# Taking the row sums of an attention chunk half a step earlier, its inverse between two clips, and the fetch of the inverse behind the last product

## The chip, the cores and the metric

The kernel runs on one core of a Trainium2 chip. A core has a matrix engine (TensorE, PE in the profile), three engines for elementwise work (VectorE or DVE, ScalarE or ACT, GpSimd or POOL), and SyncE (SP), which here only issues transfers. Each engine takes its own instructions in order, and waits on semaphores that the others raise. TensorE writes to PSUM, a small accumulator memory; the rest lives in SBUF. The metric is the device time of one launch, in microseconds (us).

## The reference

Eight graphs of 2048 nodes with 256 features go through two layers. Each layer normalises its input, clips it at zero, attends and adds the result to the input. Only the first layer is touched here. It has four heads of 64 features. Its softmax isn't taken over all 2048 keys, but within each of eight chunks of 256 keys, and the chunks' results are added:

```
scores = einsum('bhnd,bhjcd->bhnjc', q, kc) / sqrt(Dh)
scores = clip(scores, -10.0, 10.0)
scores = where(mask == 0, -10.0, scores)
attn = softmax(scores, axis=-1)          # over the 256 keys of chunk j
ctx = einsum('bhnjc,bhjcd->bhnd', attn, vc)
out = ctx @ Wo.T + bo + x                # then a layer norm with gamma, beta
```

So each query needs a sum of exponentials for each head and chunk, and each chunk's product with v has to be multiplied by the inverse of that sum before it's added to the others.

## The kernel before, in words

The first layer (`layers`, up to line 724) works in 256 steps: 8 graphs, 4 blocks of 512 queries, 8 chunks of 256 keys. A chunk is two key tiles of 128 keys, `kt` = 2c and 2c + 1. All of it is float32. For one step these instructions run:

- **Scores** (`scores`, line 396): for each key tile and each pair of heads `hp`, two matmuls on the two halves of the array's rows fill one PSUM tile `big` (two buffers). In the trace a matmul of float32 is two records, so the scores of one key tile, both pairs, are 8 records.
- **Clip** (line 404): one VectorE instruction per pair takes `big` through max and min with the mask's limits into an SBUF tile `E` of 128x1024.
- **Exponential** (`exponential`, line 410): ScalarE, in place.
- **Pair sum** (line 680): POOL adds the `E` of the two key tiles of the chunk, for each pair: `add`, two buffers.
- **Sums** (`add_up`, line 427): four matmuls with a block of ones, one per head, each on 32 of the array's columns, sum the pair sums over the keys into PSUM tile `sums`. Heads 0 and 1 read the first pair's `add`, heads 2 and 3 the second's.
- **Inverse** (`divide` and `spread`, lines 434 to 446): ScalarE copies `sums` into `s`; a transfer gathers one row per head into a tile `sum` of 128x16, VectorE takes its reciprocal, a transfer writes it to device memory (`inv`), and four transfers spread each head's row over 32 partitions of `r`, which has one buffer.
- **Products** (`weigh`, line 416): for each key tile and each half `part` of a head's features, four matmuls, one per head, on 32 columns each. Both key tiles accumulate in PSUM tile `both`, which has one buffer.
- **Accumulate** (line 452 on VectorE, line 454 on POOL): `both` times `r` into `c`, and `c` added to `acc`. The first chunk of a block goes to `acc` directly.

These aren't run for one chunk at once. The order is written out by hand in the loop after line 685: at step n TensorE makes the scores of chunk n + 2, sums the pair sums of chunk n + 1 and takes the products of chunk n. A step has two halves, `k` = 0 and 1. In each half come the scores of one key tile of chunk n + 2, then the products of one key tile of chunk n; in the second half the sums of chunk n + 1 stand between the two groups of products. `prepared` is a generator that yields after each part of chunk n + 2, so that its last part (the second pair's exponential and the two pair sums) is issued at the end of the step.

At the end of each half, `advance()` lets waiting side work issue one piece. Side work is: making q, k and v of the next graph (`block`: transposes at line 171, projections at 297 and 191), finishing a block of queries (`finish`: output projection at 479, statistics, normalisation, and POOL's additions at 469 and 512), a graph's statistics, and the start of the second layer. I call the two places slot 1 and slot 2 below, by their order in a step. In `finish`, the step after a block's last chunk runs four ScalarE activations (466) and one POOL addition (469); the next one the output projection in both slots; the one after that a square root (127), for which ScalarE loads another activation table and then loads the exponential's again.

SP issues all the transfers of this layer but the stores of finished blocks, in order: the gather of sums, the write of inverses, the four spreads of `r`, and the loads of x.

The second layer (from line 724) isn't touched.

Of the kernel before, what the change touches and what calls it, by code (L numbers as in the profile page):

```python
# [8 lines left out]
F32 = mybir.dt.float32  # L9
# [7 lines left out]
P = 128  # L17
# [10 lines left out]
def bcast(ap, axis, n):  # L28

    ap = ap.unsqueeze(axis)  # L30
    shape = list(ap.shape)
    shape[axis] = n
    return ap.broadcast_to(shape)
# [18 lines left out]
def layers(  # L52
# [22 lines left out]
    QB = 512  # L75
# [3 lines left out]
    NCH = N // 256  # L79
# [6 lines left out]
    psum = ctx.enter_context(tc.tile_pool(name="psum", bufs=1, space=PSUM))  # L86
# [12 lines left out]
    def heads_tile(name, tag, bufs=2):  # L99
        return big.tile([P, 2, QB], F32, tag=tag, name=name, bufs=bufs)  # L100
# [100 lines left out]
    aside = []  # L201
    here = [0]

    def advance():

        moved = False
        for steps_of in list(aside):
            got = next(steps_of, aside)
            if got is aside:
                aside.remove(steps_of)  # L210
            moved = moved or got is not False
            if got is None:
                break
        return moved

    def drain(until=lambda: False):
        while not until() and advance():
            pass
# [52 lines left out]
    def other_limits():  # L271
        for qb in range(1, NQB):
            yield from make_limit(qb)

    qkv, norm_of = {}, {}
# [43 lines left out]
    def batch(b):  # L319
        qkv[b] = ([], [], [])  # L320
        if b == 0:
            mv, rstd, off = norms()
            norm_of[b] = rstd, off
            for blk, xb in enumerate(ahead(x[b])):
                if blk == 0:
                    yield True
                for t in range(NT):
                    row_stats(nc, small, mv[:, blk * NT + t, :], xb[:, t, :])
                of = slice(blk * NT, (blk + 1) * NT)
                roots(mv, rstd, off, of)  # L330
                offsets(rstd, off, of)
                yield from block(b, blk, xb, *qkv[b])
        else:
            norm_of[b] = yield from statistics(x[b])
            for blk, xb in enumerate(ahead(x[b])):
                yield from block(b, blk, xb, *qkv[b])
# [5 lines left out]
    for name, w in (("q", Wq), ("k", Wk), ("v", Wv), ("o", Wo)):  # L342
# [4 lines left out]
        if name == "o":  # L347

            got = big.tile([P, FC, F], F32, tag="c", name="w_halves")
# [41 lines left out]
    def scores(qb, kt, hp, qs, ks):  # L391

        ps = psum.tile([P, 2, QB], F32, tag="big", name="big", bufs=2)
        for hh in range(2):
            own = slice(hh * DH, (hh + 1) * DH)
            nc.tensor.matmul(  # L396
                ps[:, hh, :],
                ks[kt // NT][own, hp, (kt % NT) * P : (kt % NT + 1) * P],
                qs[qb][own, hp, :],
                start=True,  # L400
                stop=True,
            )
        e = heads_tile("E", "E", 10)
        nc.vector.scalar_tensor_tensor(  # L404
            e, ps, -0.5, bcast(limit[:, qb, kt, :], 1, 2), ALU.max, ALU.min
        )
        return e

    def exponential(e):
        nc.scalar.activation(e, e, AF.Exp, scale=0.25 * EDGE)  # L410

    def weigh(kt, part, es, vs, both, first):

        for h in range(H):
            mine = slice(h * DH + 32 * part, h * DH + 32 * part + 32)
            nc.tensor.matmul(  # L416
                both[32 * h : 32 * h + 32, part, :],
                vs[kt // NT][:, kt % NT, mine],
                es[h // 2][:, h % 2, :],
                start=first,  # L420
                stop=not first,
            )

    def add_up(es, sums):

        for h in range(H):
            nc.tensor.matmul(  # L427
                sums[32 * h : 32 * h + 32, :], ones, es[h // 2][:, h % 2, :], start=True, stop=True
            )

    def divide(sums):

        s = big.tile([P, QB], F32, tag="s", name="s", bufs=1)
        nc.scalar.copy(s, sums)  # L434
        got = small.tile([P, 16], F32, tag="sum", name="sum")
        nc.sync.dma_start(got, s[0:P:32, :].rearrange("h (j i) -> h j i", i=16))
        return got

    def spread(got):

        nc.vector.reciprocal(got, got)
        held = dram.tile([H, QB], F32, tag="inv", name="inv", bufs=3)
        nc.sync.dma_start(held.rearrange("h (j i) -> (h j) i", i=16), got)
        r = big.tile([P, QB], F32, tag="r", name="r", bufs=1)
        for h in range(H):
            nc.sync.dma_start(r[32 * h : 32 * h + 32, :], held[h, :].partition_broadcast(32))
        return r

    def accumulate(acc, both, r, first):

        to = acc if first else heads_tile("c", "c")
        nc.vector.tensor_tensor(to, both, bcast(r, 1, 2), ALU.mult)  # L452
        if not first:
            nc.gpsimd.tensor_tensor(acc, acc, to, ALU.add)  # L454
# [186 lines left out]
    def fill(qb):  # L641

        while here[0] < (B - 1) * NQB * NCH + qb * NCH + NCH - 1:
            yield False
        for two in range(NKT // 2):
            mine = limit[:, qb, 2 * two : 2 * two + 2, :]
            nc.scalar.activation(mine, mine, AF.Relu, scale=2.0 * FULL, saturate=False)
            yield True

    def last_batch():  # L650
        yield from batch(B - 1)
        yield from sources_of(W, a)
        yield from preparation(0)
# [7 lines left out]
    accs = {}  # L661

    def prepared(step):


        b, qb, c = step
        drain(lambda: qb in made and b in qkv and len(qkv[b][1]) > c // 2)
        qs, ks, _ = qkv[b]
        first = [scores(qb, 2 * c, hp, qs, ks) for hp in range(2)]
        for e in first:  # L670
            exponential(e)
        yield first
        second = [scores(qb, 2 * c + 1, hp, qs, ks) for hp in range(2)]
        exponential(second[0])
        yield second
        exponential(second[1])
        added = []
        for hp in range(2):
            both = heads_tile("add", "add")
            nc.gpsimd.tensor_tensor(both, first[hp], second[hp], ALU.add)  # L680
            added.append(both)
        yield added


    weights, rs, got = {}, {}, None
    for n in range(-2, len(steps)):
        here[0] = n
        more = n < NCH - 1
        coming = prepared(steps[n + 2]) if n + 2 < len(steps) else iter(())
        inside = -1 <= n < len(steps) - 1  # L690
        if n >= 0:
            b, qb, c = steps[n]
            if n == 0:
                aside.append(other_limits())
            if (qb, c) == (0, 2) and b + 1 < B:
                aside.append(batch(b + 1) if b + 2 < B else last_batch())
            if b == B - 1 and c == NCH - 2:
                aside.append(fill(qb))
            drain(lambda: len(qkv[b][2]) > c // 2)
            early[0] = False  # L700
            both = psum.tile([P, 2, QB], F32, tag="both", name="both")
        for k in range(2):
            weights.setdefault(n + 2, []).append(next(coming, None))
            if more:
                advance()
            if n >= 0:
                weigh(2 * c + k, 0, weights[n][k], qkv[b][2], both, k == 0)
            if k == 1 and inside:
                sums = psum.tile([P, QB], F32, tag="sums", name="sums")
                add_up(weights[n + 1][2], sums)  # L710
                got = divide(sums)
            if n >= 0:
                weigh(2 * c + k, 1, weights[n][k], qkv[b][2], both, k == 0)
            if k == 0 and got:
                rs[n] = spread(got)
                got = None
            if k == 1:
                weights[n + 2].append(next(coming, None))
                if n >= 0:
                    if c == 0:  # L720
                        accs[qb] = heads_tile("acc", "acc")
                    accumulate(accs[qb], both, rs.pop(n), c == 0)
                    weights.pop(n)
                    if c == NCH - 1:
                        aside.insert(0, finish(b, qb, accs[qb]))
            advance()


    inverse_most = const.tile([P, 4 * B], F32, tag="most", name="most")
# [122 lines left out]
    due, ts, acc, den = [], None, None, None  # L852
    for s, (k, jt) in enumerate(rounds):
        here[0] = len(steps) + s // 4
        b, hp, half = passes[k]
        qn, held, off_s, far, quot, for_sums = shared[b]
# [3 lines left out]
        if jt == 0:  # L860
            acc = psum.tile([P, 2, QB], F32, tag="both", name="acc1")
# [339 lines left out]
```

## Time and profile before

| | |
|---|---|
| median of 3 runs | 4478.36 us (4476.7 to 4484.94) |
| profiled execution | 4470.84 us |
| its span, first to last instruction | 4469.0 us |
| the first layer's steps | about 125 to 2905 us of the span |
| PE busy | 4235.0 us, 95% |
| POOL busy | 3275.9 us, 73% |
| DVE busy | 3157.1 us, 71% |
| ACT busy | 2712.5 us, 61% |

All times of the prediction are from this one profiled execution. A row of the groups is: line, engine, operation, tile written and tile read, shapes, count, busy time, mean of one. In the timeline a row begins with the start in us from the span's start and the length in us, and can hold several instructions of one group; what stands in brackets at its end is the engine's idle time just before, and what ended it. PEld is the load of weights that goes ahead of a matmul. TensorE's ends are modelled, so lengths of consecutive groups of matmuls overlap a little; the distance from one start to the next is the better measure of what a group takes.

### The profile page before, as it was taken

What the parts mean: (1) busy time and instruction counts of PE and PEld (TensorE: products, weight loads), DVE (VectorE), ACT (ScalarE), POOL (GpSimd) and SP (SyncE); (2) the same over time, 40 slices, a digit from 0 to 9 for tenths busy, and PEclk for the clock granted to TensorE, in tenths of its full rate; (3) what the DMA queues carried; (4) which work ended last, traced back from release to release, by engine and by line L of the source; (5) the groups of instructions that cost most, each with busy time, mean ns of one, the idle gap of its engine ahead of it and who ended that gap; (6) DMA issues with size and microseconds to landing.
All of it is one profiled execution on the core that took longest, in us unless ns stands there. A gap on an engine that the chain in (4) does not pass through costs nothing. (4 is left out here: it accounts for less than half of the span.)

```text
span 4469.0 us, 73769 instructions
## 1 busy us (share of the span) xinstructions
PE 4235.0 (95%) x28598; PEld 1462.8 (33%) x28598; DVE 3157.1 (71%) x3736; ACT 2712.5 (61%) x3454; POOL 3275.9 (73%) x1558
## 2 busy tenths in 40 slices
PE   6799999999999999999999999989999999999998
PEld 3233333323323333333333333323233332323332
DVE  1775566566565565575565566588989889898987
ACT  4766556656655665665656557565647566565755
POOL 0477787787677777777777777777877777787877
PEclk8999999999999999999999999999999999999999
DMA  2421121111121121121111122121221212122111
GB/s 70 140 62 44 43 66 47 43 56 56 35 64 54 37 66 44 46 64 44 47 55 50 40 64 61 44 100 50 72 63 60 78 57 86 52 74 62 59 55 35
DMA packets 295000, 262.03 MB, mean 59 GB/s; under 512 B 96240, under 2 KB 245488, under 8 KB 294640
## 3 DMA queue, kind: packets, MB, share of 16 engines
q1 hardware_dynamic: 290032, 240.45, 18.8%
q0 software_dynamic: 4608, 16.78, 1.0%
q8 instruction: 226, 3.70, 0.3%
q14 instruction: 134, 1.10, 0.1%
HBM read 218.83 MB, written 36.18 MB: 57 GB/s over the span
## 5 line engine op out<-in xcount | busy, mean ns | idle before, releaser
L680 POOL TENSOR_TENSOR add<-E 128x1024 f32<-128x1024 f32 x512 | 1201.3, 2369 | 721.9 <-PE sums L427 532.1
L410 ACT ACTIVATE E<-E 128x1024 f32<-128x1024 f32 x1024 | 1080.5, 1057 | 827.3 <-DVE E L404 809.6
L404 DVE SCALAR_TENSOR_TENSOR E<-big,limit 128x1024 f32<-128x1024 f32 x1024 | 1203.7, 1217 | 521.6 <-PE big L396 515.5
L761 DVE SCALAR_TENSOR_TENSOR e<-near,far,limit 128x1024 f32<-128x1024 f32 x1024 | 1240.0, 1273 | 23.2 <-ACT near L750 9.8
L878 POOL TENSOR_TENSOR t<-t,e 128x1024 f32<-128x1024 f32 x448 | 1054.4, 2387 | 246.0 <-ACT t L874 210.4
L416 PE MATMUL both<-E,v 128*32 128x512 f32 x8192 | 1037.7, 601 | 59.8 <-DVE c L452 42.3
L772 PE MATMUL acc<-e,qn 128*32 128x512 f32 x8192 | 1060.7, 597 | 24.4 <-DVE e L761 13.5
L396 PE MATMUL big<-qT,kT 64*128 64x512 f32 x4096 | 1032.3, 620 | 11.8 <-DVE E L404 11.8
L874 ACT ACTIVATE t<-e,quot 128x1024 f32<-128x1024 f32 x512 | 561.2, 1142 | 313.5 <-PE den L784 173.0
L396 PEld LDWEIGHTS big<-qT,kT 64*128 64x128 f32 x4096 | 351.6, 187 | 572.0 <-issue 348.8
L454 POOL TENSOR_TENSOR acc<-acc,c 128x1024 f32<-128x1024 f32 x224 | 532.9, 2379 | 3.6 <-DVE c L452 3.6
L452 DVE TENSOR_TENSOR c<-both,r 128x1024 f32<-128x1024 f32 x224 | 274.2, 1224 | 345.9 <-PE both L416 157.1
L416 PEld LDWEIGHTS both<-E,v 128*32 128x32 f32 x8192 | 214.7, 109 | 752.3 <-issue 572.8
L772 PEld LDWEIGHTS acc<-e,qn 128*32 128x32 f32 x8192 | 259.2, 109 | 591.5 <-issue 451.1
L784 PE MATMUL den<-t,for_sums 128*32 128x512 f32 x2048 | 347.6, 595 | 30.6 <-POOL t L878 29.8
L427 PE MATMUL sums<-add,ones 128*32 128x512 f32 x2048 | 269.1, 592 | 0.2 <-POOL add L680 0.2
L434 ACT COPY s<-sums 128x512 f32<-128x512 f32 x256 | 148.4, 580 | 75.5 <-PE sums L427 71.3
L784 PEld LDWEIGHTS den<-t,for_sums 128*32 128x32 f32 x2048 | 79.2, 110 | 223.1 <-issue 113.3
L191 PE MATMUL aux<-w,hT 128*128 128x256 f32 x512 | 127.6, 392 | 22.6 <-DVE qn L629 22.6
L160 ACT ACTIVATE h<-x,off,rstd 128x256 f32<-128x256 f32 x256 | 139.2, 593 | 4.3 <-DMA x<-in_x_dram 2.3
L297 PE MATMUL aux<-hT,wq 128*128 128x512 f32 x256 | 135.7, 658 | 2.7 <-ACT hT L172 2.7
L479 PE MATMUL aux<-wo,acc 128*128 128x256 f32 x512 | 128.2, 393 | 0.0
(117 smaller groups left out, 3033.8 us busy)
## 6 DMA issues: line engine op xcount, KB each, us to landing
r<-inv SPq DMA_DIRECT2D x1024, 64.0 KB
x<-in_x_dram SPq DMA_DIRECT2D x92, 512.0 KB
x<-x SPq DMA_DIRECT2D x64, 512.0 KB
es<-er SPq DMA_DIRECT2D x64, 512.0 KB
adj_in<-in_adj_dram SPq DMA_DIRECT2D x32, 512.0 KB
x<-o POOLq DMA_DIRECT2D x32, 512.0 KB, 3.9
xh<-x SPq DMA_DIRECT2D x64, 256.0 KB
out_dram<-xh SPq DMA_DIRECT2D x64, 256.0 KB
```

Of the source, the lines that this page charges most:

```text
L396: nc.tensor.matmul(ps[:, hh, :], ks[kt // NT][own, hp, (kt % NT) * P : (kt % NT + 1) * P], qs[qb][own, hp, :], start=True, stop=True,)
L404: nc.vector.scalar_tensor_tensor(e, ps, -0.5, bcast(limit[:, qb, kt, :], 1, 2), ALU.max, ALU.min)
L410: nc.scalar.activation(e, e, AF.Exp, scale=0.25 * EDGE)
L416: nc.tensor.matmul(both[32 * h : 32 * h + 32, part, :], vs[kt // NT][:, kt % NT, mine], es[h // 2][:, h % 2, :], start=first, stop=not first,)
L452: nc.vector.tensor_tensor(to, both, bcast(r, 1, 2), ALU.mult)
L454: nc.gpsimd.tensor_tensor(acc, acc, to, ALU.add)
L680: nc.gpsimd.tensor_tensor(both, first[hp], second[hp], ALU.add)
L761: nc.vector.scalar_tensor_tensor(e, near[hh], far[:, jt, h : h + 1], limit[:, 2 * half : 2 * half + 2, jt, :], ALU.max, ALU.min,)
L772: nc.tensor.matmul(acc[32 * q : 32 * q + 32, blk, :], qn[jt // NT][:, jt % NT, hp * P + 32 * q : hp * P + 32 * q + 32], es[q // 2][:, blk, :],
L784: nc.tensor.matmul(den[32 * q : 32 * q + 32, :], for_sums[:, m, 2 * hp + q // 2, :], ts[q // 2][:, q % 2, :], start=(m == 0 and k == 0), s ...
L874: nc.scalar.activation(t, now[hh], AF.Copy, scale=quot[:, jt // 2, h : h + 1])
L878: nc.gpsimd.tensor_tensor(ts[hh], ts[hh], now[hh], ALU.add)
```

## The change

The loop over `k` is written out, and four things move:

- The sums of chunk n + 1, with the copy and the gather, stand between the two groups of products of the first key tile, not of the second. They come before the exponentials of the first key tile of chunk n + 2, which `prepared` now issues after its first yield.
- The scores of the second key tile are issued in two parts, and the reciprocal and the write of `inv` (now `inverse_of`) stand between them, so that VectorE takes the reciprocal between the clips of the two pairs. Before, they came in the next step, after both clips of its first key tile.
- The products of the second key tile are eight matmuls in a row.
- The four spreads of `r` (`spread`) are issued at the end of the step, after the accumulate of chunk n, which reads the one buffer of `r`. Before, they came in the first half of the step that uses them.

The pair sums stay at the end of the step, and nothing is added or taken away.

```diff
+    def inverse_of(got):
         nc.vector.reciprocal(got, got)
         held = dram.tile([H, QB], F32, tag="inv", name="inv", bufs=3)
         nc.sync.dma_start(held.rearrange("h (j i) -> (h j) i", i=16), got)
+        return held
+
+    def spread(held):
         r = big.tile([P, QB], F32, tag="r", name="r", bufs=1)
...
         first = [scores(qb, 2 * c, hp, qs, ks) for hp in range(2)]
+        yield first
         for e in first:
             exponential(e)
-        yield first
-        second = [scores(qb, 2 * c + 1, hp, qs, ks) for hp in range(2)]
+        yield
+        second = [scores(qb, 2 * c + 1, 0, qs, ks)]
+        yield
+        second.append(scores(qb, 2 * c + 1, 1, qs, ks))
         exponential(second[0])
         yield second
         exponential(second[1])
...
-        for k in range(2):
-            weights.setdefault(n + 2, []).append(next(coming, None))
-            if more:
-                advance()
-            if n >= 0:
-                weigh(2 * c + k, 0, weights[n][k], qkv[b][2], both, k == 0)
-            if k == 1 and inside:
-                sums = psum.tile([P, QB], F32, tag="sums", name="sums")
-                add_up(weights[n + 1][2], sums)
-                got = divide(sums)
-            if n >= 0:
-                weigh(2 * c + k, 1, weights[n][k], qkv[b][2], both, k == 0)
-            if k == 0 and got:
-                rs[n] = spread(got)
-                got = None
...
+        weights[n + 2] = [next(coming, None)]
...
+            weigh(2 * c, 0, weights[n][0], qkv[b][2], both, True)
+        got = held = None
+        if inside:
+            sums = psum.tile([P, QB], F32, tag="sums", name="sums")
+            add_up(weights[n + 1][2], sums)
+            got = divide(sums)
+        next(coming, None)
+        if n >= 0:
+            weigh(2 * c, 1, weights[n][0], qkv[b][2], both, True)
+        advance()
+        next(coming, None)
+        if got:
+            held = inverse_of(got)
+        weights[n + 2].append(next(coming, None))
...
+            for part in range(2):
+                weigh(2 * c + 1, part, weights[n][1], qkv[b][2], both, False)
+        weights[n + 2].append(next(coming, None))
...
+            accumulate(accs[qb], both, r, c == 0)
...
+        if held:
+            r = spread(held)
+        advance()
```

More of the change, by code (lines that the diff above doesn't have):

```diff
@@ L437, in divide @@
         return got
-    def spread(got):
+    def inverse_of(got):
         nc.vector.reciprocal(got, got)
@@ L682, in prepared @@
         yield added
-    weights, rs, got = {}, {}, None
+    weights = {}
     for n in range(-2, len(steps)):
@@ L701, in layers @@
             both = psum.tile([P, 2, QB], F32, tag="both", name="both")
-        for k in range(2):
-            weights.setdefault(n + 2, []).append(next(coming, None))
-            if more:
-                advance()
-            if n >= 0:
-                weigh(2 * c + k, 0, weights[n][k], qkv[b][2], both, k == 0)
-            if k == 1 and inside:
-                sums = psum.tile([P, QB], F32, tag="sums", name="sums")
-                add_up(weights[n + 1][2], sums)
-                got = divide(sums)
-            if n >= 0:
-                weigh(2 * c + k, 1, weights[n][k], qkv[b][2], both, k == 0)
-            if k == 0 and got:
-                rs[n] = spread(got)
-                got = None
[L717 to L725, printed above, removed]
-            advance()
+        weights[n + 2] = [next(coming, None)]
@@ new lines, in layers @@
+        if more:
+            advance()
+        if n >= 0:
[6 more added lines that the diff above has]
+        next(coming, None)
+        if n >= 0:
+            weigh(2 * c, 1, weights[n][0], qkv[b][2], both, True)
[3 more added lines that the diff above has]
+            held = inverse_of(got)
@@ new lines, in layers @@
+        weights[n + 2].append(next(coming, None))
+        if more:
+            advance()
+        if n >= 0:
+            for part in range(2):
+                weigh(2 * c + 1, part, weights[n][1], qkv[b][2], both, False)
+        weights[n + 2].append(next(coming, None))
+        if n >= 0:
+            if c == 0:
+                accs[qb] = heads_tile("acc", "acc")
+            accumulate(accs[qb], both, r, c == 0)
+            weights.pop(n)
+            if c == NCH - 1:
+                aside.insert(0, finish(b, qb, accs[qb]))
@@ L729, in layers @@
+        if held:
+            r = spread(held)
+        advance()
     inverse_most = const.tile([P, 4 * B], F32, tag="most", name="most")
```

## The prediction

> **What bounds the kernel now.** I read the page first, then the busy times of the first layer alone, then who waited for whom there, and last the timeline of one step without side work. The change touches only the first layer.
>
> ```profile
> span 4469.0 us, 73769 instructions
> PE 4235.0 (95%) x28598; PEld 1462.8 (33%) x28598; DVE 3157.1 (71%) x3736; ACT 2712.5 (61%) x3454; POOL 3275.9 (73%) x1558
> ```
>
> TensorE is the bound. The stretch of the first layer says how much of it is idle (columns: stretch, length, then busy time and instructions of PE, PEld, DVE, ACT, POOL):
>
> ```profile
> 140.00:2910.00 2770.00, 2671.64 (x16198) 923.98 (x16196) 1735.56 (x2170) 1688.91 (x2132) 2035.28 (x934) 1.00 0.19 55
> ```
>
> PE idles 2770.0 - 2671.6 = 98 us in 256 steps. That is the ceiling of any gain here. The waits of that stretch (engine, line, what it waited for: total us, times, longest):
>
> ```profile
> DVE c L452 <- DMA r<-inv: 136.1, 67, 3.8
> ...
> DVE acc L452 <- DMA r<-inv: 43.2, 17, 4.6
> PE both L416 <- DVE c L452: 42.3, 52, 2.7
> ...
> PE both L416 <- DVE acc L452: 17.3, 12, 3.2
> ...
> PE big L396 <- DVE E L404: 11.1, 28, 2.6
> ```
>
> So `r` comes late, the accumulate waits, and PE waits for the one buffer of `both`: 42.3 + 17.3 = 59.6 us, with 11.1 us of late clips behind it. These 71 us are what the change can win. Now one step (rows between left out):
>
> ```profile
> 1581.02 1.92 PE L416 MATMUL both<-E,v 128*32 128x512 f32 x16
> ...
> 1582.88 1.99 PE L396 MATMUL big<-qT,kT 64*128 64x512 f32 x8
> ...
> 1584.12 2.36 DVE L404 SCALAR_TENSOR_TENSOR E<-big,limit 128x1024 f32<-128x1024 f32 x2 [1.18 <-PE big L396]
> ...
> 1584.79 1.07 PE L416 MATMUL both<-E,v 128*32 128x512 f32 x8
> ...
> 1585.38 1.06 ACT L410 ACTIVATE E<-E 128x1024 f32<-128x1024 f32 x1 [1.50 <-DVE E L404]
> 1585.68 1.04 PE L427 MATMUL sums<-add,ones 128*32 128x512 f32 x8
> ...
> 1586.54 1.04 PE L416 MATMUL both<-E,v 128*32 128x512 f32 x8
> ...
> 1586.86 0.59 ACT L434 COPY s<-sums 128x512 f32<-128x512 f32 x1 [0.42 <-PE sums L427]
> 1586.89 4.69 POOL L680 TENSOR_TENSOR add<-E 128x1024 f32<-128x1024 f32 x2 [1.37 <-PE sums L427]
> ...
> 1587.51 1.99 PE L396 MATMUL big<-qT,kT 64*128 64x512 f32 x8
> ...
> 1588.81 1.22 DVE L452 TENSOR_TENSOR c<-both,r 128x1024 f32<-128x1024 f32 x1 [2.33 <-DMA r<-inv]
> ...
> 1590.08 1.92 PE L416 MATMUL both<-E,v 128*32 128x512 f32 x16 [0.59 <-DVE c L452]
> ```
>
> Start to start, eight score records take 1.91 us, sixteen product records 1.86, eight 0.89, the sums 0.86, the last products 0.97. The second scores start at 1582.88, their first clip 1.24 later, the exponential of that pair at 2.50, done at 3.56; the two pair sums then take 4.69. They are read by the sums of the *second* half of the next step, with time to spare: in the whole span PE waited 0.2 us for them, its weight loads 3.3.
>
> **The Trainium skill.** "TensorE: Matmul & The Clock Gate", section "The mechanism", says that matmuls start and end strictly in order; here a wait at the sums therefore holds everything behind them. The trace agrees: no product starts before the sums ahead of it. "GPSIMD Engine Reference", section "Elementwise — side-by-side cycle accounting", gives 4497 ns for an addition of 2048 float32 per partition on GpSimd and 1.96 times less on VectorE; half of that is an estimate of 2.25 us for our 1024, and the trace has 2.37 us: the pair sums are slow, and there are two in a row. "DMA: Bandwidth & Descriptors", section "Anatomy of one DMA — SWDGE (gpsimd) path", fits a fixed cost of about 2.0 us to a transfer on GpSimd's own queue; SP's small write of `inv` shows less, 1.4 us from its issue at 1516.03 to that of the spread waiting for it at 1517.45.
>
> **The change, part by part.**
>
> *Removed: the wait for `r`.* The reciprocal comes a good half step sooner, and the spreads start when the accumulate has read the old `r`. The accumulate starts 1.16 us after the last group of products (1512.36 after 1511.20) and takes 1.22; four issues take 1.7 us, and the page gives even a store of 512 KB 3.9 us to land, so `r`, 64 KB in each transfer, is there within an estimated 6 us of the accumulate's end, and the next accumulate is at least 8.40 - 1.22 = 7.2 us away (8.40 us is a step without side work, 1649.27 to 1657.67). Gain: the 71 us, between 60 and the ceiling of 98. The spreads now wait on SP for the accumulate, and only a load of x or the next gather is behind them: no cost.
>
> *Moved with a cost: the sums.* Let T be the start of the second key tile's scores. Until the next sums PE then has: scores 1.91, sixteen products 1.86, slot 2, scores 1.91, four products 0.89: T + 6.57 + slot 2. The pair sums end, by the row times, at 3.56 + 0.13 (elsewhere in the timeline an exponential ends at 1596.76 and the addition waiting for it starts at 1596.89) + 4.69 = T + 8.38; they can't start sooner, for the first exponential is done only at 3.56. Adding 0.06 us to wake PE (an accumulate ends at 1601.06, the product waiting for it starts at 1601.12), heads 2 and 3 start at T + 8.44. PE waits 8.44 - 6.57 = 1.87 us minus slot 2; I take 1.85. Nothing carries over, as the following chain starts from the delayed sums. If the first two heads' matmuls, 0.4 us, run inside the wait, it is 1.46; the records show both passes of four heads interleaved and weight loads one round ahead, so I take the upper value.
>
> In the built order of the changed kernel, slot 2 of 94 steps holds no TensorE work, 32 hold four transposes (0.59 us, 1520.57 to 1521.16), 4 a projection for the second layer (0.9, an estimate), and nearly all the rest a projection of 1.92 us (1499.92 to 1501.84), which just covers it. Cost: 94 x 1.85 + 32 x 1.26 + 4 x 0.95 = 174 + 40 + 4 = 218 us. With 1.46: 137 + 28 + 2 = 167 us.
>
> *What delays the pair sums further.* The copy of `s` starts 1.18 us after the sums (1586.86), then come the two first exponentials, which formerly ran before it (0.48 later, 2.19 for both): ScalarE is free 3.85 us after the sums. The next exponential could start 0.86 + 0.97 + 2.50 = 4.33 after them, plus slot 1: 0.5 us of cover. Two pieces of `finish` in slot 1 exceed it. In the step after a block's last chunk, four activations (2.07 us, 1536.73) end at 5.9, then POOL's addition of 2.37 ends at 8.3, where the pair sums were due at 5.5 plus slot 1: 2.8 us. Of four blocks of a graph three have no TensorE work in slot 1 there, and one has both slots full (0.9): 3 x 2.8 + 0.9 = 9.3 us per graph, 8 graphs: 75 us. Two steps later come the square root and two table loads (from 1561.18 to the exponential at 1564.75, about 3 us): 2.5 us minus slot 1. Of four blocks one has nothing in slot 1, two have transposes (1.9) and one a projection (0.6), the rest of it offset by slot 2: 2.5 + 1.8 + 1.8 + 0.5 = 6.6 us, times 8 = 53 us. Formerly the same delays met the spare half step. Bounds: none of it, to all 128 us.
>
> *At nothing:* the reciprocal between the clips. Its gather is issued 1.8 us after the sums and lands some 2 us later (an estimate from 1.4 us above), while the first clip ends 0.86 + 0.97 + 2.43 = 4.26 after them. It puts 0.24 us before the second clip, whose exponential ends 1.1 us before POOL comes to it. Without that cover it costs at most the 0.24. The eight products in a row and the two-part scores are the same instructions, and neither adds a change of array shape.
>
> Sum: -71 + 218 + 75 + 53 = +275 us on the span of 4469.0, or 4744. The profiled execution took 1.8 us more than its span, and the median is 7.5 us above that execution: 4478.4 + 275 = 4753 us.
>
> **Rivals.**
> *A, the waits without the side work's delays:* `finish` hides behind the wait itself. 4478 - 71 + 218 = 4625 us. For it: PE's own pause delays everything and gives ScalarE time. Against: the chain is counted from the sums, after the pause.
> *B, the wait is shorter as well:* 1.46 us for each, 4478 - 71 + 167 = 4574 us.
> *C, faster:* the sums aren't late, `r` is early, and the kernel wins the 71 us: 4407 us. Its one mechanism is pair sums that end before PE comes to heads 2 and 3. It decides where the chain ends before T + 6.57 plus slot 2: the chain would have to be 1.9 us shorter, or the mean wait below 71 / 256 = 0.28 us. Against it is every row above; for it only that the profile of before, where the sums came later, can't show the wait itself.
> *D, worse:* a late gather holds the second clip too, and SP's spreads delay the loads of x for `finish`: 30 to 100 us more, 4780 to 4850 us.
>
> **How the numbers follow.** The likeliest, 4753 us, has 0.58, within 4680 to 4810; A 0.18, B 0.10, C 0.06, D 0.08. From B's 4574 to the lower half of D at 4830 the range leaves out C, the lower half of B and half of D: about 0.15. All cases but C are slower by over 0.2%, about what a measurement of this kernel can tell from no change: slower 0.93, same 0.01, faster 0.06.
>
> **What would show it.** In the profile after, the waits of the accumulate for `r` are gone, and so are those of PE for the accumulate. In their place TensorE (or its weight loads) waits for POOL's `add` at the sums, some 130 to 170 times at about 1.8 us, 290 to 350 us in all, longest 4 to 5 us in the step after a block's last chunk; a step without side work takes 10.2 us. PE's idle time in this layer grows from 98 to over 350 us. The second layer takes the same time. I am wrong if the pair sums end less than 7 us after the second key tile's scores start, or if PE passes on to products while heads 2 and 3 wait.

## The result and the profile after

| | before | after |
|---|---|---|
| median of 5 runs each | 4478.36 us | 4759.42 us (4753.73 to 4761.23) |
| ratio to before | 1 | 1.0623, 95% interval 1.0609 to 1.0638 |
| span of the profiled execution | 4469.0 us | 4758.5 us |
| from the end of the first layer's last accumulate to the end | 1564.6 us | 1560.6 us |

The change makes the kernel 6.2% slower, 281 us. All of it is in the first layer, whose last accumulate starts at 2903.2 us in the profile of before and at 3196.7 us in that of after.

From the page of the kernel after, the first two lines and the row of the sums:

```profile
span 4758.5 us, 73841 instructions
...
PE 4406.9 (93%) x28598; PEld 1486.1 (31%) x28598; DVE 3151.1 (66%) x3736; ACT 2681.4 (56%) x3454; POOL 3271.3 (69%) x1558
...
L427 PE MATMUL sums<-add,ones 128*32 128x512 f32 x2048 | 443.7, 610 | 186.2 <-POOL add L686 186.2
```

The same 28598 matmul records; only their order is new. The other engines' busy times are those of before within 32 us. At the sums TensorE was idle for 0.2 us in all before, and is now for 186 us, waiting for POOL. (POOL's pair sum is line 686 now.) The waits of the first layer of the kernel after:

```profile
PEld sums L427 <- POOL add L686: 414.5, 371, 4.7
...
PE sums L427 <- POOL add L686: 182.5, 182, 3.8
...
POOL o L472 <- ACT o L469: 111.9, 31, 7.7
...
DVE c L455 <- PE both L416: 19.4, 70, 1.2
```

No wait for `r` is left among them, neither of the accumulate for the transfer (179 us before) nor of TensorE for the accumulate (60 us). What the change set out to remove is gone. In its place TensorE stands at the sums. Its weight loads, which run one round ahead of the matmuls, show the pause more fully than the matmuls do, for the first two of the four heads still run in it. The third row is the addition of `finish`, which waits 112 us for ScalarE; before, it waited 30 in the same layer.

One wait in the timeline of the kernel after, with nothing in slot 2 (TensorE's rows, then POOL's):

```profile
1643.44 1.99 PE L396 MATMUL big<-qT,kT 64*128 64x512 f32 x8
1645.36 1.92 PE L416 MATMUL both<-E,v 128*32 128x512 f32 x16
1647.22 1.99 PE L396 MATMUL big<-qT,kT 64*128 64x512 f32 x8
1649.13 1.06 PE L416 MATMUL both<-E,v 128*32 128x512 f32 x8
1650.02 1.03 PE L427 MATMUL sums<-add,ones 128*32 128x512 f32 x4
1651.88 0.62 PE L427 MATMUL sums<-add,ones 128*32 128x512 f32 x2 [0.83 <-POOL add L686]
1651.89 0.62 PE L416 MATMUL both<-E,v 128*32 128x512 f32 x2
...
1653.72 1.99 PE L396 MATMUL big<-qT,kT 64*128 64x512 f32 x8
```

```profile
1647.14 4.69 POOL L686 TENSOR_TENSOR add<-E 128x1024 f32<-128x1024 f32 x2 [2.92 <-ACT E L410]
1651.78 2.37 POOL L457 TENSOR_TENSOR acc<-acc,c 128x1024 f32<-128x1024 f32 x1
```

The second key tile's scores start at 1643.44. TensorE reaches the sums 6.58 us later, at 1650.02, and runs both passes of heads 0 and 1. POOL starts its two additions at 1647.14, 3.70 after the scores, because the exponential isn't done sooner, and ends them at 1651.83. Heads 2 and 3 start at 1651.88, 8.44 us after the scores. The step takes 10.28 us instead of 8.40.

### The profile page after: what moved, and what is told of

Its sections match the earlier page's. It is cut to its first block, busy times and chain, and to the rows that moved or that the text cites. A ratio compares the mean times of both kernels' runs of the same rounds, so it can differ in the third digit from the quotient of the medians.

```text
span 4758.5 us, 73841 instructions
## 1 busy us (share of the span) xinstructions
PE 4406.9 (93%) x28598; PEld 1486.1 (31%) x28598; DVE 3151.1 (66%) x3736; ACT 2681.4 (56%) x3454; POOL 3271.3 (69%) x1558
## 5 line engine op out<-in xcount | busy, mean ns | idle before, releaser
L410 ACT ACTIVATE E<-E 128x1024 f32<-128x1024 f32 x1024 | 1047.3, 1054 | 272.3 <-DVE E L404 269.9
L416 PE MATMUL both<-E,v 128*32 128x512 f32 x8192 | 1187.7, 605 | 0.1
L396 PE MATMUL big<-qT,kT 64*128 64x512 f32 x4096 | 1021.0, 617 | 3.8 <-DVE E L404 3.8
L427 PE MATMUL sums<-add,ones 128*32 128x512 f32 x2048 | 443.7, 610 | 186.2 <-POOL add L686 186.2
L416 PEld LDWEIGHTS both<-E,v 128*32 128x32 f32 x8192 | 236.2, 109 | 694.9 <-issue 647.1
L427 PEld LDWEIGHTS sums<-add,ones 128*32 128x32 f32 x2048 | 87.9, 109 | 493.7 <-POOL add L686 421.7
L490 DVE TENSOR_TENSOR o<-o,aux 128x512 f32<-128x512 f32 x64 | 43.4, 678 | 193.0 <-issue 171.4
L472 POOL TENSOR_TENSOR o<-o,ro 128x1024 f32<-128x1024 f32 x32 | 76.0, 2374 | 118.6 <-ACT o L469 118.6
```

What stands on the lines that cost most here:

```text
L396: nc.tensor.matmul(ps[:, hh, :], ks[kt // NT][own, hp, (kt % NT) * P : (kt % NT + 1) * P], qs[qb][own, hp, :], start=True, stop=True,)
L416: nc.tensor.matmul(both[32 * h : 32 * h + 32, part, :], vs[kt // NT][:, kt % NT, mine], es[h // 2][:, h % 2, :], start=first, stop=not first,)
L427: nc.tensor.matmul(sums[32 * h : 32 * h + 32, :], ones, es[h // 2][:, h % 2, :], start=True, stop=True)
```

## Experiments

Each was run beside the kernel before on the same chip, and the ratio to it has its 95% interval behind it. The changed kernel was measured at another time, when the kernel before stood 3 to 7 us higher. Differences to the changed kernel are between those medians; taken from the ratios they would be 4 to 10 us smaller.

### The early sums without the pair sums

```diff
-            add_up(weights[n + 1][2], sums)
+            add_up(weights[n + 1][0], sums)
```

> The changed kernel, with one edit: the ones-matmuls at their early place read the exponentials of the chunk's first key tile instead of the pair sums, so the second key tile is left out of the softmax's sums. POOL still makes the pair sums, but nobody waits for them. The number and shapes of TensorE's instructions stay the same. Theory (TensorE waits at the early sums for POOL's pair sums, and for nothing else that is new): the wait goes and the early inverse remains, so the 59.6 + 11.1 us of the kernel before are won: 4407 us, within 4385 to 4440. Rival (the loss comes from the new order on ScalarE and VectorE, the exponentials behind the copy and the reciprocal between the clips, which this edit leaves as it is): above 4700 us.

Measured: 4428.11 us beside 4475.69, ratio 0.9895 (0.9878 to 0.9911). With the wait for POOL taken away and all the rest of the change in place the kernel is 47.6 us faster than before, and 331 us faster than the changed kernel. So the whole loss hangs on this one dependency: without it, the new order on ScalarE and VectorE makes nothing slower than before. It isn't free, though. The expected gain was 71 us; this run's waits of TensorE say what remained:

```profile
PE aux L171 <- ACT h L160: 27.2, 22, 3.0
PE aux L260 <- ACT masks L248: 14.1, 11, 3.6
PE big L396 <- DVE E L404: 13.9, 12, 4.9
```

All three exist in the kernel before too, and the second, side work, is about as long there (16.4 us). The first is not. It is TensorE's transposes of the next graph's normalised input `h`, which ScalarE makes. In the first layer of the kernel before it was:

```profile
PE aux L171 <- ACT h L160: 2.3, 5, 1.1
```

So it grew by some 24 us, about what is missing of the gain (71 - 47.6 = 23 us). In this run `h` stands on ScalarE behind the activations of `finish`, and in the longest of these waits they in turn wait for a load of x: 33.0 us in all, 7.6 before. The loads are issued by SP, whose order the change altered as well. This is read from the rows; no run took it away.

The third, scores that wait for a clip, was 11.1 us before and was to go. One such place, VectorE's and SP's rows of the same run:

```profile
1560.29 1.22 DVE L404 SCALAR_TENSOR_TENSOR E<-big,limit 128x1024 f32<-128x1024 f32 x1 [2.20 <-PE big L396]
1563.74 0.25 DVE L440 RECIPROCAL sum<-sum 128x16 f32<-128x16 f32 x1 [2.23 <-DMA sum<-s]
1563.91 1.16 DVE L404 SCALAR_TENSOR_TENSOR E<-big,limit 128x1024 f32<-128x1024 f32 x1
```

```profile
1558.57 0.98 SPq L104 DMA_DIRECT2D x<-in_x_dram  x2
1559.65 0.56 SPq L436 DMA_DIRECT2D sum<-s  x1
```

The gather, issued just behind two loads of 512 KB, is used 4.1 us after its issue, not after the 2 us that I had estimated, and the reciprocal between the clips holds the second clip for 2.2 us. In the whole run 35 reciprocals waited for their gather. For 28 of them SP had issued a load of x less than 2.5 us before the gather, and the median from issue to use is 3.5 us; for the other seven it is 1.9 us.

### The exponentials ahead of the early sums again

```diff
         first = [scores(qb, 2 * c, hp, qs, ks) for hp in range(2)]
-        yield first
         for e in first:
             exponential(e)
+        yield first
         yield
```

> The changed kernel with the exponentials of the first key tile issued before the early sums and their copy again, as in the kernel before; all else as changed. Theory: the plain wait for the pair sums stays (some 220 us), but ScalarE is free 2.1 us sooner, so that the activations and the POOL addition of a finished block and the square root with its two table loads delay the pair sums by 0.7 and 0.5 us instead of 2.8 and 2.5: some 106 us less, 4653 us, within 4630 to 4690. Rival A (the side work hides behind the wait and costs nothing): 4759 us, within 15. Rival of the new order on ScalarE as the cause of the whole loss: about 4410 to 4480 us.

Measured: 4660.25 us, ratio 1.0410 (1.0392 to 1.0427): 99 us less than the changed kernel, where 106 were expected. So the side work's delays are real, and nearly all of them come from ScalarE's order. The plain wait remains: of the 281 us, 185 are still there. The waits of TensorE at the sums and of POOL's addition in `finish` in this run:

```profile
PE sums L427 <- POOL add L686: 127.8, 151, 2.7
...
POOL o L472 <- ACT o L469: 72.1, 31, 7.5
```

The longest fell from 3.8 to 2.7 us, and POOL's wait for the activations from 112 to 72 us.

### The first piece of a block's finish in slot 2

```diff
         while here[0] < n + 1:
             yield False
+        yield False
         o = big.tile([P, NT, F], F32, tag="o", name="o")
```

> The changed kernel with the first piece of a block's finish (four activations and one POOL addition) moved from slot 1 to slot 2 of the same step, where it stands behind the pair sums on POOL and not ahead of them. Theory: the 9.3 us per graph of that step, 75 us in all, go: 4684 us, within 4660 to 4705. Rival A (they are hidden): 4759 us, within 15.

Measured: 4691.32 us, ratio 1.0480 (1.0462 to 1.0497): 68 us less than the changed kernel, where 75 were expected. A piece of work that runs once in eight steps, moved half a step, is worth 1.5% here.

### The reciprocal behind both clips

```diff
-        if got:
-            held = inverse_of(got)
         weights[n + 2].append(next(coming, None))
+        if got:
+            held = inverse_of(got)
```

> The changed kernel with the reciprocal and the write of the inverse behind both clips of the second key tile, not between them. Theory: the place of the reciprocal costs nothing and wins nothing, since the inverse has several us to spare either way: 4759 us, within 10. Rival (a late gather holds the second clip and with it the second pair sum): faster by 0.24 us and more per step, below 4700 us.

Measured: 4760.91 us, ratio 1.0637 (1.0619 to 1.0655). To within the 8 us of this interval the place of the reciprocal costs nothing and wins nothing in the changed kernel.

### The same without the pause that could hide it

The edits of the first experiment and of the one just above together; the second key tile is left out of the sums here too.

> The run that leaves the second key tile out of the sums, with the reciprocal moved behind both clips as well. There TensorE has no pause that could hide anything. Theory: a gather that comes late behind two loads of x held the second clip and through it the scores, 13.9 us in that run, and this goes: 4414 us against 4428, within 4405 to 4420. Rival (the place of the reciprocal costs nothing with or without cover): 4428 us, within 4.

Measured: 4424.73 us beside 4471.47, ratio 0.9896 (0.9881 to 0.9911), against 0.9895. A miss: the clips' wait did shrink, from 13.9 to 2.6 us, but TensorE then waited 6.5 us for the accumulate, which it hadn't done, and the time didn't move. The intervals reach 7 us to either side, so the 5 us that are left of those 11 couldn't be seen. The late gather of the first run's timeline is there, but removing it isn't worth anything that can be measured. The transposes' wait for `h` is as long as in the first run (27.4 us).

### The second pair's sum on VectorE

```diff
         for hp in range(2):
+            if hp == 1:
+                yield added
             both = heads_tile("add", "add")
-            nc.gpsimd.tensor_tensor(both, first[hp], second[hp], ALU.add)
+            engine = nc.vector if hp else nc.gpsimd
+            engine.tensor_tensor(both, first[hp], second[hp], ALU.add)
             added.append(both)
-        yield added
+        yield
...
             if c == NCH - 1:
                 aside.insert(0, finish(b, qb, accs[qb]))
+        next(coming, None)
         if held:
             r = spread(held)
```

> The changed kernel with the second pair's sum (1024 of 2048 columns of a chunk) on VectorE, issued after the accumulate, instead of behind the first pair's on POOL. Theory (two POOL additions in a row are what the early sums wait for): the first pair's sum ends 6.0 us after the second key tile's scores start, the second's about 6.4, both ahead of TensorE's arrival at 6.6 plus slot 2; the waits at the sums nearly go, and VectorE's additional 1.2 us a step costs something where statistics share the step: 4430 us, within 4400 to 4480. Rival (the sums are too early for any engine, or VectorE becomes the bound): above 4550 us.

Measured: 4616.55 us, ratio 1.0324 (1.0310 to 1.0338). Of the 281 us, 145 are left, so about half is won back. That is far above the expected range and within the rival's. VectorE hasn't become the bound: it is busy for 80% of this run's span, TensorE for 95%. The rows of the tiles `add` and `acc` show what I had wrong (minimum, median and maximum in ns):

```profile
L689 POOL TENSOR_TENSOR add<-E x256: 2343/2362/3341, 121.8 to 3037.1; 128x1024 f32<-128x1024 f32 x128
L689 DVE TENSOR_TENSOR add<-E x256: 1215/2087/4460, 122.9 to 3038.5; 128x1024 f32<-128x1024 f32 x128
```

```profile
L457 POOL TENSOR_TENSOR acc<-acc,c x224: 2333/3361/3389, 156.8 to 3055.3; 128x1024 f32<-128x1024 f32 x112
```

I had priced VectorE's addition at 1.22 us. Its minimum is that, but its median is 2.09 and its worst 4.46; POOL's addition to `acc` went from a median of 2.38 to 3.36. The Trainium skill has this: "SBUF — State Buffer", section "Summary: rules for kernel authors", says that when VectorE has two SBUF inputs and GpSimd's operation reads SBUF, the second one to be issued blocks until the first is done. The trace agrees. One place:

```profile
1506.23 2.36 POOL L689 TENSOR_TENSOR add<-E 128x1024 f32<-128x1024 f32 x1 [1.02 <-ACT E L410]
...
1507.63 2.04 DVE L689 TENSOR_TENSOR add<-E 128x1024 f32<-128x1024 f32 x1
1508.55 3.36 POOL L457 TENSOR_TENSOR acc<-acc,c 128x1024 f32<-128x1024 f32 x1
```

POOL's first addition ends at 1508.59 us, VectorE's 1.08 us later, and POOL's next addition takes 1 us longer than usual. Of the 256 additions on VectorE 251 took over 1.3 us, each of them began while an instruction of POOL was running, and 245 ended 1.08 or 1.09 us after that instruction had ended. So the two nearly always take turns. The second pair's sum therefore ended 7.2 us after the second key tile's scores in the median, not 6.4, and so behind TensorE's arrival, at 6.6 where slot 2 is empty. That this accounts for the whole 145 us is not shown, since the side work's delays are in them too. The accumulate itself, with one input in PSUM, keeps its 1.22 us throughout.

### The kernel before with the reciprocal between two clips

The sums stay in the second half; the scores of the first key tile are issued in two parts, and the reciprocal and the write of the inverse stand between their clips. `spread` is split as in the change, and its transfers stay where they were.

```diff
-        first = [scores(qb, 2 * c, hp, qs, ks) for hp in range(2)]
+        first = [scores(qb, 2 * c, 0, qs, ks)]
+        yield
+        first.append(scores(qb, 2 * c, 1, qs, ks))
...
         for k in range(2):
+            if k == 0:
+                next(coming, None)
+                if got:
+                    got = inverse_of(got)
             weights.setdefault(n + 2, []).append(next(coming, None))
```

> The kernel before, with its sums in the second half of the step, and one thing of the change: the reciprocal and the write of the inverse stand between the two clips of the next step's first key tile, not behind both. Theory: the inverse comes about 1.2 us sooner, most of the accumulate's waits for it (mean 2.1 us, 84 of them) shrink, and most of TensorE's 59.6 us go without any wait at the sums: 4430 us, within 4415 to 4455. Rival (the wait for the inverse can't be shortened without moving the sums): 4476 us, within 8.

Measured: 4440.45 us beside 4471.47, ratio 0.9932 (0.9918 to 0.9945). This beats both kernels, by 31 us and by some 310 to 320. TensorE's wait for the accumulate and the accumulate's for `r`, in this run:

```profile
PE both L416 <- DVE acc L454: 9.2, 13, 1.9
...
PE both L416 <- DVE c L454: 5.8, 12, 1.4
```

```profile
DVE c L454 <- DMA r<-inv: 43.9, 25, 2.3
...
DVE acc L454 <- DMA r<-inv: 25.9, 9, 4.4
```

Of TensorE's 59.6 us 15.0 are left, and of the accumulate's 179 us 70. One small instruction and the write behind it, moved by one clip, get two thirds of what the early sums could have won (31 of 47.6 us), and no wait for POOL comes with it: 0.3 us.

### And the sums ahead of all the second key tile's products

```diff
-            if n >= 0:
-                weigh(2 * c + k, 0, weights[n][k], qkv[b][2], both, k == 0)
             if k == 1 and inside:
...
             if n >= 0:
+                weigh(2 * c + k, 0, weights[n][k], qkv[b][2], both, k == 0)
                 weigh(2 * c + k, 1, weights[n][k], qkv[b][2], both, k == 0)
```

> As the run with the kernel before and the reciprocal between the first clips, and the sums one group of products earlier too: ahead of the eight products of the second key tile, behind its scores. Theory: the pair sums still have about 1.9 us plus both slots to spare, the gather comes 0.9 us sooner, so the inverse is hardly ever late: 4420 us, within 4405 to 4445; not slower than the run without that step by more than 10 us. Rival (each step that the sums are moved forward costs a wait for POOL): above 4450 us.

Measured: 4440.37 us, ratio 0.9932 (0.9919 to 0.9946), the same as without it. The sums 0.9 us sooner still wait for POOL only 1.1 us in all, and TensorE's wait for the accumulate falls from 15.0 to 9.4 us, but the time doesn't follow. So moving the sums isn't harmful as such. It cost nothing here, where they still came after the end of the pair sums, and 331 us in the change, where they passed it.

## Why the prediction was right

- **The bound and the ceiling.** Right. TensorE is the bound before and after, and no variant beat the kernel before by as much as the 98 us of idle time.
- **The wait for `r` goes.** Right. In the changed kernel all of TensorE's 59.6 us for the accumulate are gone, and its wait for late clips fell from 11.1 to 2.4 us. The size was put at 71 us. The run without POOL's wait won only 47.6; in its rows the transposes wait some 24 us longer than before, and the clips are no less late.
- **The chain of the pair sums.** Right to the hundredth in a plain step: TensorE arrives 6.58 us after the scores (6.57 predicted), heads 2 and 3 start at 8.44 (8.44 predicted), and the step takes 10.28 us (10.2 predicted). The choice between 1.46 and 1.85 us for the wait was right, but its reason was not. The prediction took the upper value because both passes of four heads are interleaved, as if heads 0 and 1 would wait too. They do run inside the pause, from 1650.02 on. What keeps the pause whole is that the next scores come 1.84 us after the release, as they would without a pause, though half of the sums are done by then. The prediction didn't have this, so that the 51 us between its two sums (218 and 167) fell on the right side by luck.
- **The side work's delays.** Right: 106 us for the order on ScalarE measured 99, 75 us for the first piece of `finish` measured 68. The square root's part wasn't run alone. Rival A, which had them hidden, is out.
- **The sum of the costs.** Measured by the run without POOL's wait, the costs are 331 us against 218 + 75 + 53 = 346, and the gain 47.6 against 71. A second count is an estimate from the starts in the profiles: the distance from one group of TensorE's records to the next, less what the same two groups take where nothing waits (the 5th percentile over all ten profiles). Around the sums this lost time rose from about 7 to 375 us, and elsewhere in the first layer it fell from about 114 to 37. That is a cost of some 367 us and a gain of some 77, and their difference, 290 us, is what the span grew by. The counts differ because the pause covers waits that come to light without it, such as the transposes' (27.2 us without, 6.5 in the changed kernel). In both counts the errors of the terms cancel in part. So the net, 281 us against 275, is closer than the working could promise.
- **At nothing.** Right for the reciprocal, in the changed kernel and without the pause. Its reason was not quite: in the run without POOL's wait the gather, put at 2 us, takes 4.1 when two loads of x are ahead of it on SP, and the second clip does wait. In the changed kernel the reciprocal waits for its gather three times, 5.5 us in all. Case D had named the late gather and late loads of x. Both show in the runs without POOL's wait, but the changed kernel stayed below D's 4780 us. That the new order on SP costs nothing is likewise right only for the changed kernel.
- **What the profile would show.** The waits for `r` went and those at the sums came, but the rows of waits don't give their size: 130 to 170 waits of 290 to 350 us in all were named, and TensorE's row has 182 with 182.5 us, its weight loads' 371 with 414.5 us. By the starts, as above, some 160 steps stand still, 375 us in all, and twelve of them for over 5 us, where 4 to 5 had been named for the longest. PE's idle time is far off: 350 us and more were named for the first layer, and its stretch of 3060 us shows 211.6 us (2848.4 busy). The rest is in PE's busy time, which rose by 172 us over the whole run with the same matmuls: in the step above, the four records of heads 0 and 1 count as 1.03 us of work inside a pause of 1.86 us. "Trainium Kernel Development and Optimization", section "Performance Expectations", in the Trainium skill calls matmul busy time a bad metric for the distance to roofline, since matmuls are pipelined. Here it misleads in a way of its own: a slower order looks busier. The weight loads' row is the nearer one, though it also counts their lead of about 0.3 us where nothing stands still.

## What to carry to other kernels

An operand that is consumed sooner has to be produced sooner: before a consumer is moved forward, add up its producer's chain from the last instruction both share, and compare it with what the in-order engine does in between. Here that is 8.44 us against 6.57, and everything behind the sums paid for the difference, while two thirds of the gain were to be had by moving one small instruction on the late path itself. An engine's pause covers some waits of others, here the transposes'. It isn't free cover when their chain begins only after the pause: what delays the chain came on top nearly in full, 99 of 106 us and 68 of 75.

## What wasn't expected of the hardware

- A VectorE addition of two SBUF operands beside POOL additions: 2.09 us in the median and up to 4.46, against a minimum of 1.22. POOL's addition to `acc` went from 2.38 to 3.36 us. In 245 of 256 cases VectorE's ended 1.08 or 1.09 us after the POOL instruction that ran when it began.
- A gather of 8 KB behind two loads of 512 KB on the same issuing engine took 4.1 us from its issue to its use. Of the gathers that were waited for, those behind such loads took 3.5 us in the median and the others 1.9.
- A wait in the middle of a group of four column-tiled matmuls splits it: two heads run both their passes alone, and the other two share the array with the next group's first two (1651.88 and 1651.89). The pause keeps its full length.
